# A tuned cross-attention and feed-forward kernel: the short chunk of the score maxima taken out of the score loop, with a new order in the opening

## The chip, the cores and the metric

The kernel runs on one core of one Trainium2 chip. The metric is the device time of one execution in microseconds (us), as the median of several runs; lower is better. A core has a matrix engine (TensorE, in profiles PE, with its weight loads as PEld), a vector engine (VectorE, DVE), an engine for activation functions (ScalarE, ACT), a general engine (GpSimd, POOL) and SyncE (SP), which issues transfers. Each works through its own list of instructions in order and waits on semaphores for the others.

## The reference

`x` has 2048 rows of 256, the context 1601 rows of 192 with a mask, and there are 16 heads of 64. A null key and a null value are put in front, so there are 1602 keys. All is float32.

```python
x = layer_norm(x, g_norm)                  # of a layer norm of the input
q = x @ Wq
k, v = jnp.split(context @ Wkv, 2, axis=-1)
...
k = jnp.concatenate([nk, k], axis=2)       # null key and value in front
v = jnp.concatenate([nv, v], axis=2)
sim = jnp.einsum('bhid,bhjd->bhij', q * sqrt_scale, k * sqrt_scale)
sim = jnp.where(full_mask[:, None, None, :], sim, max_neg)
attn = jax.nn.softmax(sim, axis=-1)
out = jnp.einsum('bhij,bhjd->bhid', attn, v)
...
return layer_norm(out @ Wout, g_out)
```

The result is added to `x`, and then a feed-forward part with three layers of signs (256 twice to 1024, 1024, 256; ReLU between) of a layer norm of the sum is added as well.

## The kernel before

Two heads form a pair, and 512 rows of `x` a block: 8 pairs times 4 blocks are 32 *units*, numbered u = 4p + b. Keys lie in 13 tiles of 128 (`KC`), the last of them with 66 rows. Every engine's list is written out by hand in program order (`manual_schedule`), so a line's place in the code is its place in the queue of its engine.

A unit has three stretches.

- **The score loop** (L709 to L722), k = 0 to 12. `exps` computes transposed scores of one key tile for both heads (`scores`, L442: two matmuls of a 64-row half of the array each, each in two fp32 passes) and ScalarE takes the exponential (L468). For k = 0 and 1 a matmul L466 puts in the shifts, later tiles build on the scores before them in the same PSUM buffer through stepped keys (`keys_stepped`). There are two score buffers (`spare`, the pool `ps_s`). In the same step one chunk of the row maxima of the *next* unit is computed: `max_chunk` multiplies 128 queries with 512 keys for both heads in fp32r (L400) and VectorE reduces (L403). Four query tiles times three chunks make 12 of these, and the thirteenth is the short chunk `REST`: the last 66 keys for all four query tiles, eight matmuls of 64 rows and 66 columns (L384) and one reduce (L387). `order` puts it into step 11. The maxima use the other PSUM pool with two buffers (`flex`, the pool `ps_f`), which also holds `den`, `mt`, the projections of queries, keys and values and, in the first units, the turned input. GpSimd sums the exponentials into `acc` (L720, L722, L728). A copy of one element of the last unit's `acc` on ScalarE (L711, `seen`) stands in step 2 or 8; ScalarE goes no further before that `acc` is complete.
- **The weighted sum** (L752, L475): 104 matmuls in four column groups. Ahead of it stand the denominators of the unit before, in the form of four quarters (`denominators`, L499, and `divided_quarters`), or within it in the whole form (`divided`, L524) in units 1, 30 and 31. GpSimd adds the remaining exponentials to `acc`.
- **The tail** (L782 to L800): the maxima are turned (`max_turned`, L413), the unit before is projected to the output (`project_out`, L488; VectorE adds it into `y_sb`, L491 and L493, which frees the buffer `po`), the queries of the unit after next are projected (`project_q`, L211, with ScalarE writing `qr` and `qT`, L212 and L213), and a quarter of the next pair's keys and values (`project_k`, L270 and L275; `project_v`, L305 and L320). `round_k` (L289) makes the fp32r copy `kr` of the keys for the maxima.

Each unit's maxima must be complete a unit ahead, since its shifts come from them.

Before the first unit, the *opening* (L566 to L678) loads everything, normalises blocks 0 and 1 of `x`, projects the first pair's keys, queries and values and computes the maxima of unit 0. Blocks 2 and 3 are normalised in units 0 and 1 (`input_normed` with `centred_beside`, ScalarE), for `input_turned` in the tail of the same unit. `masked_counted` (L425) computes `spent`, by which ScalarE scales the first exponentials' rows (L726). After the last unit the feed-forward part follows (L836, L867).

Of the kernel before, what the change touches and what calls it, by code (L numbers as in the profile page):

```python
# [38 lines left out]
def xattn_ffn(ctx, tc, x, ctxT, mask, g_norm, null_kv, wq, wkv, wout, g_out, k0, k1, k2, s0, s1, s2, out):  # L39
# [108 lines left out]
    with ExitStack() as att:  # L148
# [17 lines left out]
        mcol = ap.tile([128, 128], F32, name="mcol")  # L166
        pick = ap.tile([128, 4, 1], F32, name="pick")
# [66 lines left out]
        def first_keys(n, get, part=None):  # L234
# [3 lines left out]
            if part != 1:  # L238
                halves["k"] = get(f"psk_0_{n}")
# [6 lines left out]
            if part == 0:  # L246
                return
# [5 lines left out]
            for i, (start, w) in enumerate(chunks):  # L253
                for part in range(2 if n == 0 else 1):
                    keys = ds(256 * part, 256) if n == 0 else ds(start, w)
                    relative(kT, ps[:, i, ts(part, 256)] if n == 0 else ps[:, i, :w], keys)
                    if n == 0 and part == 0:
# [6 lines left out]
        def project_k(p, m):  # L264
# [3 lines left out]
            ps = flex(f"psk_{p}_{m}")  # L268
            for i in range(2):
                nc.tensor.matmul(  # L270
                    ps[:, i, :w], weights[p][1][:, 0, :], ctx_a[:, ds(start + i * w, w)], start=True, stop=False
                )
            for i in range(2):
# [10 lines left out]
        def round_k(p, m):  # L284

            kT, _, kr = pairs[p]
            start, w = HALF_KEYS[m]
            keys = ds(start, 2 * w)
            nc.scalar.copy(kr[:, keys], kT[:, keys])  # L289

# [8 lines left out]

        def values_begun(p, m, tiles, get=flex):  # L300
# [3 lines left out]
            for t in tiles:  # L304
                nc.tensor.matmul(  # L305
                    halves[p, m][:, t - 8 * m, :],
                    ctx_a[:, ts(t, 128)],
                    weights[p][1][:, 1, :],
                    start=t % 4 == 0,
# [4 lines left out]
        def values_ended(p, m):  # L314
# [3 lines left out]
            for t in sorted(tiles, key=lambda t: (t % 4, t)):  # L318
                rows = ts((t - 8 * m) // 4, 64)
                nc.tensor.matmul(  # L320
                    pv[:, t - 8 * m, :],
# [6 lines left out]
            w = len(tiles)  # L328
            nc.scalar.copy(v[:, ds(8 * m, w), :], pv[:, :w, :])
# [46 lines left out]
        def max_chunk(p, b, n, get=flex):  # L376
            ps = get(f"max_{p}_{b}_{n}")
            qr, kr = queries[p, b][1], pairs[p][2]
            if n == REST:
                start, w = CHUNKS[3]  # L380
                for t in range(4):
                    for j in range(2):
                        rows = ts(j, DH)
                        nc.tensor.matmul(  # L384
                            ps[:, j, ts(t, w)], qr[rows, ts(t, 128)], kr[rows, ds(start, w)], start=True, stop=True
                        )
                nc.vector.tensor_reduce(  # L387
                    maxima[p, b][:, :, :, 3].rearrange("p t j -> p j t"),
                    ps[:, :, : 4 * w].rearrange("p j (t k) -> p j t k", k=w),
# [5 lines left out]
            if n == 0:  # L395
                maxima[p, b] = wp.tile([128, 4, 2, 4], F32, tag="mx", name=f"mx_{p}_{b}")
# [167 lines left out]
        order = (*range(REST - 1), REST, REST - 1)  # L564
# [56 lines left out]
        nc.gpsimd.memset(mcol, 0.0)  # L621
        nc.gpsimd.memset(kept, 0.0)
# [331 lines left out]
```

## Time and profile before

| what | value |
|---|---|
| median of 3 runs | 1270.56 us (1269.84 to 1270.65) |
| time of the profiled execution | 1270.18 us |
| its span, first to last instruction | 1268.4 us |
| clock granted to TensorE | 1.0 |
| attention units, first score of unit 0 to the end of unit 31's weighted sum | 31.1 to 1079.0 us |
| four consecutive units (first score of unit 5 to that of unit 9) | 132.1 us |
| bytes moved by DMA | 13.46 MB |

How such lines are read: in a group of instructions or in a timeline, a line names the start, the length, the engine, the line of the kernel, the operation, output and inputs with their shapes and how many instructions were merged ("x4"). In square brackets stands how long the engine had been idle before, and what ended the wait. "64\*128" is the part of the array that a matmul uses, rows by columns. A merged line's length runs from its first start to its last end, so that the difference between starts says more of a rate than a length does. All times are in microseconds from the first instruction. DMA plays no part after the first 20 us.

```profile
PE   8999999999999999999999999999999999999998
POOL 5898999899889988998899988998898999701100
DMA  6000000000000000000000000000000010000000
```

These are rows of the page that cuts the span into 40 equal slices, with each digit the busy share in tenths: TensorE and GpSimd are busy throughout the attention units, DMA only at the start.

### The profile page before, as it was taken

How to read it: one execution, taken by the hardware profiler on the slowest of the kernel's cores; microseconds unless marked ns; L12 is line 12 of the kernel's file. 1: busy time of each engine (PE TensorE's matmuls, PEld its weight loads, DVE VectorE, ACT ScalarE, POOL GpSimd, SP SyncE). 2: the span in 40 equal slices, each digit the busy share in tenths (PEclk: the TensorE clock that was granted, in tenths of full speed). 3: DMA queues.
4: the chain of work that ended last, by engine and by line, in shares of the span. 5: the costliest groups of instructions: out<-in, count | busy, mean ns of one | idle time of the engine just before them, and what ended most of it. 6: DMA issues, size and time to landing. Idle time of an engine off the chain costs nothing.

```text
span 1268.4 us, 19642 instructions
## 1 busy us (share of the span) xinstructions
PE 1257.9 (99%) x8332; PEld 644.0 (51%) x8332; DVE 761.7 (60%) x812; ACT 717.9 (57%) x982; POOL 1008.5 (80%) x515
## 2 busy tenths in 40 slices
PE   8999999999999999999999999999999999999998
PEld 5344444444444444444444444444444443788887
DVE  6687766656665566556655666656666793635431
ACT  4776666666666656665666566666666676322120
POOL 5898999899889988998899988998898999701100
PEclk9999999999999999999999999999999999999999
DMA  6000000000000000000000000000000010000000
GB/s 171 1 1 5 1 1 13 5 1 1 13 5 1 1 14 5 1 1 13 5 1 2 13 5 1 1 1 6 1 17 1 1 42 1 1 17 1 17 17 17
DMA packets 16984, 13.46 MB, mean 11 GB/s; under 512 B 3152, under 2 KB 16336, under 8 KB 16896
## 3 DMA queue, kind: packets, MB, share of 16 engines
q1 hardware_dynamic: 15904, 11.21, 3.2%
q8 instruction: 65, 1.06, 0.4%
q10 hardware_dynamic: 656, 0.79, 0.2%
q0 software_dynamic: 336, 0.21, 0.1%
q14 instruction: 23, 0.19, 0.0%
HBM read 10.11 MB, written 2.10 MB: 10 GB/s over the span
## 4 chain that ended last, share of the span: by engine, by line
PE 95%; POOL 2%; ACT 1%; DMA 1%; issue 0%; DVE 0%; SPq 0%; DVEq 0%; POOLq 0%; ACTq 0%
PE sT L442 28%; PE av L475 27%; PE ps L836 12%; PE max L400 7%; PE psq L211 4%; PE po L488 4%; PE ps L867 2%; PE psv L305 2%; PE psk L270 1%; PE den L499 1%; PE sT L466 1%; PE psv L320 1%; POOL acc L728 1%; PE psk L275 1%; PE max L384 1%; PE mt L413 1%
## 5 line engine op out<-in xcount | busy, mean ns | idle before, releaser
L403 DVE TENSOR_REDUCE mx<-max 128x2 f32<-128x1024 f32 x384 | 444.4, 1218 | 86.0 <-PE max L400 82.3
L728 POOL TENSOR_TENSOR acc<-acc,e 128x1024 f32<-128x1024 f32 x192 | 473.1, 2464 | 15.1
L468 ACT ACTIVATE e<-sT 128x1024 f32<-128x1024 f32 x416 | 425.8, 1024 | 87.7 <-PE sT L466 44.3
L442 PE MATMUL sT<-qT,kT 64*128 64x512 f32 x1664 | 444.8, 608 | 1.6 <-ACT e L468 1.3
L722 POOL TENSOR_TENSOR acc<-acc,e 128x1024 f32<-128x1024 f32 x160 | 379.3, 2371 | 12.6
L475 PE MATMUL av<-e,v 128*32 128x512 f32 x3328 | 363.6, 592 | 0.1
L400 PE MATMUL max<-kr,qr 64*128 64x512 f32 x768 | 280.6, 718 | 1.2 <-ACT qr L227 1.0
L475 PEld LDWEIGHTS av<-e,v 128*32 128x32 f32 x3328 | 107.4, 110 | 237.9 <-issue 230.1
L442 PEld LDWEIGHTS sT<-qT,kT 64*128 64x128 f32 x1664 | 134.0, 185 | 132.6 <-ACT e L468 121.0
L720 POOL TENSOR_TENSOR acc<-e,e 128x1024 f32<-128x1024 f32 x32 | 75.6, 2363 | 59.6 <-ACT e L468 59.6
L400 PEld LDWEIGHTS max<-kr,qr 64*128 64x128 f32 x768 | 76.7, 187 | 88.6 <-DVE mx L403 65.2
L517 ACT COPY aoT<-r 32x256 f32<-32x256 f32 x224 | 90.2, 403 | 33.4 <-DVE r L511 31.1
L782 ACT COPY avs<-av 128x512 f32<-128x512 f32 x32 | 18.8, 587 | 145.8 <-PE av L475 145.8
L415 DVE TENSOR_TENSOR mT<-mt,pick 128x512 fp32r<-128x512 f32 x32 | 22.1, 690 | 113.4 <-PE mt L413 112.9
L518 DVE TENSOR_TENSOR aoT<-avs,aoT 128x512 f32<-128x512 f32 x28 | 33.3, 1189 | 94.4 <-ACT aoT L517 94.4
L836 PE MATMUL ps<-h0hi,w 128*128 128x512 f32 x256 | 79.6, 392 | 0.0
L836 PE MATMUL ps<-h0lo,w 128*128 128x512 f32 x256 | 78.9, 389 | 0.0
L124 POOL TENSOR_TENSOR y_sb<-y_sb,gout_sb 128x256 f32<-128x256 f32 x12 | 9.3, 777 | 85.6 <-DVE y_sb L91 85.6
L824 ACT ACTIVATE h1hi<-ps 128x1024 fp32r<-128x1024 f32 x16 | 16.4, 1027 | 99.2 <-PE ps L836 99.2
L212 ACT ACTIVATE qr<-psq 128x512 fp32r<-128x512 f32 x31 | 18.5, 598 | 93.5 <-PE psq L211 91.4
L488 PE MATMUL po<-wo,aoT 128*128 128x256 f32 x256 | 60.5, 379 | 0.0
L825 DVE SCALAR_TENSOR_TENSOR h1lo<-ps,h1hi 128x1024 fp32r<-128x1024 f32 x16 | 19.6, 1224 | 67.0 <-ACT h1hi L824 67.0
(171 smaller groups left out, 1207.8 us busy)
## 6 DMA issues: line engine op xcount, KB each, us to landing
out_x<-o SPq DMA_DIRECT2D x7, 256.0 KB, 2.1
x_sb<-in_x SPq DMA_DIRECT2D x3, 512.0 KB, 5.2
wa<-in_wkv SPq DMA_DIRECT2D x8, 128.0 KB, 2.9
wb<-in_wkv SPq DMA_DIRECT2D x16, 64.0 KB, 2.5
wq<-in_wq SPq DMA_DIRECT2D x8, 128.0 KB, 2.2
wo<-in_wout SPq DMA_DIRECT2D x8, 128.0 KB, 2.1
xnT<-in_k SPq DMA_DIRECT2D x1, 1024.0 KB, 5.7
ctx_a<-in_ctxT SPq DMA_DIRECT2D x2, 256.0 KB, 6.2
```

What stands on the lines that cost most here:

```text
L211: nc.tensor.matmul(ps[:, 0, :], weights[p][0][:, c, :], xnT[:, b, c, :], start=c == 0, stop=c == 1)
L400: nc.tensor.matmul(ps[:, j, :w], qr[rows, ts(t, 128)], kr[rows, ds(start, w)], start=True, stop=True)
L403: nc.vector.tensor_reduce(maxima[p, b][:, t, :, c], ps[:, :, :w], AX.X, ALU.max)
L442: nc.tensor.matmul(ps[:n, j, :], kT[rows, ds(128 * KEY_TILES[k], n)], qT[rows, :], start=k < 2, stop=k >= 2, skip_group_check=k >= 2,)
L468: nc.scalar.activation(e, ps, AF.Exp)
L475: nc.tensor.matmul(av[ts(i, 32), 0, :], v[:n, KEY_TILES[k], ts(i, 32)], e[:n, i // 2, :], start=k == 1, stop=k == 0, tile_position=(0, 32 ...
L488: nc.tensor.matmul(pv[:, t, :], aoT[:, ts(t, 128)], weights[p][3], start=True, stop=True)
L517: nc.scalar.copy(aoT[ds(64 * j + 32 * rows, 32), ts(h, 256)], r[ds(64 * j + 32 * h, 32), :])
L720: nc.gpsimd.tensor_tensor(acc, es[1], es[2], ALU.add)
L722: nc.gpsimd.tensor_tensor(acc, acc, es[k], ALU.add)
L728: nc.gpsimd.tensor_tensor(acc, acc, es[k], ALU.add)
L836: nc.tensor.matmul(ps[:, f, :], w(c)[:, ts(2 * g + f, 128)], parts[part][:, c, :], start=i == 0, stop=i == len(steps) - 1,)
```

## The change

- **The short chunk.** A tile `apart` per pair parity holds the last 66 keys of both heads in block-diagonal form: head 0 in rows 0 to 63 and columns 0 to 65, head 1 in rows 64 to 127 and columns 66 to 131, zeros elsewhere. The short chunk is then four matmuls of 128 rows and 132 columns. It leaves the score loop: it is computed one unit earlier, in the tail, straight after the projection of the queries that it needs (behind the output projection from unit 2 on, between the two halves of the key projection in units 0 and 1). In the loop step 0 has chunk 0, step 1 none, and step k from 2 on chunk k - 1. `round_k` leaves these 66 keys out of `kr` and `keys_apart` fills `apart`.
- **The tail's order.** From unit 2 on the queries are projected before the output.
- **Balanced last values.** The five last tiles of the values lie as three and two over the two halves of the PSUM tile (`places`), so that the second part of their projection takes three tiles in the upper and two in the lower row half, instead of four and one; the copy to `v` becomes two.
- **Blocks 2 and 3** of the input are centred on GpSimd within the sums of units 0 and 1, instead of on ScalarE.
- **The copy L711** stands in step 2 in all units from 1 to 28, instead of units 3 to 27; unit 1 takes the quartered denominators.
- **The opening.** One part of the key projection moves ahead of the second block's sums and the third maximum, six of eight value tiles are begun before the maxima of chunk 1, `reciprocal` and `second_normed` move behind three of these, the load of the Exp table moves behind the values, and `masked_counted` moves to the end of unit 0's loop.

```diff
+        apart = [ap.tile([128, 2, KEYS - CHUNKS[3][0]], F32R, name=f"apart_{i}") for i in range(2)]
...
-            keys = ds(start, 2 * w)
+            keys = slice(start, min(start + 2 * w, CHUNKS[3][0]))
             nc.scalar.copy(kr[:, keys], kT[:, keys])
+            if m == 1:
+                keys_apart(p, nc.scalar.copy)
+
+        def keys_apart(p, copy):
+
+            start, w = CHUNKS[3]
+            for j in range(2):
+                copy(apart[p % 2][ts(j, DH), j, :], pairs[p][0][ts(j, DH), ds(start, w)])
...
+        places = {t: t if t < 8 else t - 8 if t < 11 else t - 7 for t in range(KC)}
...
-            for t in sorted(tiles, key=lambda t: (t % 4, t)):
-                rows = ts((t - 8 * m) // 4, 64)
+            for t in sorted(tiles, key=lambda t: (places[t] % 4, t)):
+                rows = ts(places[t] // 4, 64)
...
-            w = len(tiles)
-            nc.scalar.copy(v[:, ds(8 * m, w), :], pv[:, :w, :])
+            for at, w in ((0, 8),) if m == 0 else ((8, 3), (11, 2)):
+                nc.scalar.copy(v[:, ds(at, w), :], pv[:, ds(places[at], w), :])
...
             if n == REST:
-                start, w = CHUNKS[3]
+                w = 2 * CHUNKS[3][1]
                 for t in range(4):
-                    for j in range(2):
-                        rows = ts(j, DH)
-                        nc.tensor.matmul(
-                            ps[:, j, ts(t, w)], qr[rows, ts(t, 128)], kr[rows, ds(start, w)], start=True, stop=True
-                        )
+                    nc.tensor.matmul(
+                        ps[:, t // 2, ts(t % 2, w)],
+                        qr[:, ts(t, 128)],
+                        apart[p % 2].rearrange("p j k -> p (j k)"),
+                        start=True,
+                        stop=True,
+                    )
...
-        order = (*range(REST - 1), REST, REST - 1)
...
+        for i in range(2):
+            nc.gpsimd.memset(apart[i].bitcast(F32), 0.0)
...
+        first_keys(1, spare, 0)
         mv, r = second_summed()
         max_chunk(0, 0, 6)
-        first_keys(1, spare, 0)
+        first_keys(1, spare, 1)
         max_chunk(0, 0, 9)
-        first_keys(1, spare, 1)
-        values_begun(0, 0, range(0, 8), spare)
+        first_keys(1, spare, 2)
+        values_begun(0, 0, range(0, 6), spare)
         max_chunk(0, 0, 1)
+        max_chunk(0, 0, 4)
+        values_begun(0, 0, range(6, 8), spare)
+        values_ended(0, 0)
+        max_chunk(0, 0, 7)
         nc.vector.reciprocal(r, r)
         second_normed(mv, r)
-        nc.scalar.activation(warm, eps_sb, AF.Exp)
-        max_chunk(0, 0, 4)
-        values_ended(0, 0)
-        max_chunk(0, 0, 7)
         first_keys(3, spare)
         max_chunk(0, 0, 10)
+        max_chunk(0, 0, 2)
         values_begun(0, 1, range(8, KC), spare)
-        max_chunk(0, 0, 2)
+        max_chunk(0, 0, 5)
         values_ended(0, 1)
-        max_chunk(0, 0, 5)
+        nc.scalar.activation(warm, eps_sb, AF.Exp)
...
-        project_q(0, 1, spare)
+        project_q(0, 1, spare, 0)
         max_chunk(0, 0, REST)
+        project_q(0, 1, spare, 1)
...
+        max_chunk(0, 1, REST)
         scores(0, 0, 0, sT[0])
-        masked_counted(flex)
...
-                    if k == (2 if 2 < u < len(units) - 4 else 8) and last is not None:
+                    if k == (2 if u < len(units) - 3 else 8) and last is not None:
...
-                    if nxt is not None:
-                        max_chunk(*nxt, order[k])
+                    if nxt is not None and k != 1:
+                        max_chunk(*nxt, max(k - 1, 0))
...
+                if u == 0:
+                    masked_counted(flex)
...
+                if u < 2:
+                    mv, r = input_root(u + 2)
+                    nc.vector.reciprocal(r, r)
+                    nc.scalar.activation(warm, eps_sb, AF.Exp)
                 for k in (0, *range(8, KC)):
                     nc.gpsimd.tensor_tensor(acc, acc, es[k], ALU.add)
+                    if k == 0 and u < 2:
+                        for j in range(4):
+                            t = 4 * (u + 2) + j
+                            nc.gpsimd.tensor_scalar(
+                                y_sb[:, t, :], x_sb[:, t, :], mv[:, j, 0:1], r[:, j : j + 1], ALU.subtract, ALU.mult
+                            )
...
-                if u < 2:
-                    input_normed(u + 2, *input_root(u + 2), beside=True)
-                    nc.scalar.activation(warm, eps_sb, AF.Exp)
...
-                quarters = last is not None and u not in (1, len(units) - 2, len(units) - 1)
+                quarters = last is not None and u not in (len(units) - 2, len(units) - 1)
...
+                if u >= 2 and u + 2 < len(units):
+                    project_q(*units[u + 2])
                 if last is not None:
                     project_out(*last[:2], aoT)
-                if u + 2 < len(units):
+                if u < 2:
                     project_q(*units[u + 2])
+                if u + 2 < len(units) and u >= 2:
+                    max_chunk(*units[u + 2], REST)
                 if p + 1 < NP:
 
-                    (project_k if b < 2 else project_v)(p + 1, b % 2)
+                    if u < 2:
+                        project_k(p + 1, b, 0)
+                        max_chunk(*units[u + 2], REST)
+                        project_k(p + 1, b, 1)
+                    else:
+                        (project_k if b < 2 else project_v)(p + 1, b % 2)
```

More of the change, by code (lines that the diff above doesn't have):

```diff
@@ L237, in first_keys @@
             chunks = (CHUNKS[1], CHUNKS[2]) if n == 1 else (CHUNKS[n],)
-            if part != 1:
+            if not part:
                 halves["k"] = get(f"psk_0_{n}")
@@ L245, in first_keys @@
                     )
-            if part == 0:
+            if part in (0, 1):
                 return
@@ L256, in first_keys @@
                     relative(kT, ps[:, i, ts(part, 256)] if n == 0 else ps[:, i, :w], keys)
-                    if n == 0 and part == 0:
+                    if n == 3:
+                        keys_apart(0, nc.gpsimd.tensor_copy)
+                    elif n == 0 and part == 0:
                         nc.scalar.copy(kr[:, keys], kT[:, keys])
@@ L262, in first_keys, with project_k @@
                 nc.vector.memset(kT[:, KEYS:], 0.0)
-        def project_k(p, m):
+        def project_k(p, m, part=None):
             kT = pairs[p][0]
             start, w = HALF_KEYS[m]
-            ps = flex(f"psk_{p}_{m}")
-            for i in range(2):
+            if part != 1:
+                halves["k"] = flex(f"psk_{p}_{m}")
+            ps = halves["k"]
+            for i in range(2) if part != 1 else ():
                 nc.tensor.matmul(
@@ L272, in project_k @@
                 )
+            if part == 0:
+                return
             for i in range(2):
@@ L305, in values_begun @@
                 nc.tensor.matmul(
-                    halves[p, m][:, t - 8 * m, :],
+                    halves[p, m][:, places[t], :],
                     ctx_a[:, ts(t, 128)],
                     weights[p][1][:, 1, :],
-                    start=t % 4 == 0,
+                    start=places[t] % 4 == 0,
                     stop=False,
@@ L317, in values_ended @@
             tiles = range(8 * m, min(8 * m + 8, KC))
-            for t in sorted(tiles, key=lambda t: (t % 4, t)):
-                rows = ts((t - 8 * m) // 4, 64)
+            for t in sorted(tiles, key=lambda t: (places[t] % 4, t)):
+                rows = ts(places[t] // 4, 64)
                 nc.tensor.matmul(
-                    pv[:, t - 8 * m, :],
+                    pv[:, places[t], :],
                     ctx_b[rows, ts(t, 128)],
@@ L378, in max_chunk @@
             qr, kr = queries[p, b][1], pairs[p][2]
+            if (p, b) not in maxima:
+                maxima[p, b] = wp.tile([128, 4, 2, 4], F32, tag="mx", name=f"mx_{p}_{b}")
             if n == REST:
-                start, w = CHUNKS[3]
+                w = 2 * CHUNKS[3][1]
                 for t in range(4):
-                    for j in range(2):
-                        rows = ts(j, DH)
-                        nc.tensor.matmul(
-                            ps[:, j, ts(t, w)], qr[rows, ts(t, 128)], kr[rows, ds(start, w)], start=True, stop=True
-                        )
+                    nc.tensor.matmul(
[5 more added lines that the diff above has]
+                    )
                 nc.vector.tensor_reduce(
-                    maxima[p, b][:, :, :, 3].rearrange("p t j -> p j t"),
-                    ps[:, :, : 4 * w].rearrange("p j (t k) -> p j t k", k=w),
+                    maxima[p, b].rearrange("p (i t) j c -> p i (t j) c", i=2)[:, :, :, 3],
+                    ps[:, :, : 2 * w].rearrange("p i (t k) -> p i t k", k=w // 2),
                     AX.X,
@@ L394, in max_chunk @@
             t, c = divmod(n, 3)
-            if n == 0:
-                maxima[p, b] = wp.tile([128, 4, 2, 4], F32, tag="mx", name=f"mx_{p}_{b}")
             start, w = CHUNKS[c]
```

## The prediction

> **What bounds the kernel now.** I read the page first: busy shares and the chain that ended last.
>
> ```profile
> PE 1257.9 (99%) x8332; PEld 644.0 (51%) x8332; DVE 761.7 (60%) x812; ACT 717.9 (57%) x982; POOL 1008.5 (80%) x515
> PE 95%; POOL 2%; ACT 1%; DMA 1%; issue 0%; DVE 0%; SPq 0%; DVEq 0%; POOLq 0%; ACTq 0%
> ```
>
> TensorE carries the chain, but its ends are modelled, so 99% does not say it runs at full rate. Start times do. Every unit has three stretches: the score loop (13 steps), the weighted sum (104 matmuls, 0.109 us apart, 11.3 us), and a tail of projections. Next I read the timeline of unit 5 (pair 1, block 1), first the middle of its loop.
>
> ```profile
> 205.59 4.44 ACT L468 ACTIVATE e<-sT 128x1024 f32<-128x1024 f32 x4
> 205.88 4.61 DVE L403 TENSOR_REDUCE mx<-max 128x2 f32<-128x1024 f32 x4
> 206.66 0.30 PEld L442 LDWEIGHTS sT<-qT,kT 64*128 64x128 f32 x4 [0.36 <-ACT e L468]
> 207.20 0.19 PEld L400 LDWEIGHTS max<-kr,qr 64*128 64x128 f32 x2 [0.23 <-DVE mx L403]
> 207.82 0.30 PEld L442 LDWEIGHTS sT<-qT,kT 64*128 64x128 f32 x4 [0.43 <-ACT e L468]
> 208.91 0.30 PEld L442 LDWEIGHTS sT<-qT,kT 64*128 64x128 f32 x4 [0.36 <-ACT e L468]
> ```
>
> Every score load L442 waits for an exponential, two steps back, because there are two score buffers. Load starts alternate 1.16 and 1.09 apart, 2.25 for two steps. That is the sum of one closed chain: exponential 1.02, 0.05 to the load, load 0.11, two passes of 0.43, then 0.21 until the next exponential in that buffer: 2.25. The maxima of a step (one pass, 0.21) run while TensorE would wait, and are not in the chain. VectorE is as full by coincidence: its reduces start 1.13 apart without a gap. Which of the two sets the pace is told by unit 31, which computes no maxima at all; its exponentials:
>
> ```profile
> 1054.14 2.01 ACT L468 ACTIVATE e<-sT 128x1024 f32<-128x1024 f32 x2 [0.30 <-PE sT L466]
> 1056.46 2.01 ACT L468 ACTIVATE e<-sT 128x1024 f32<-128x1024 f32 x2 [0.30 <-POOL acc L728]
> 1058.77 2.01 ACT L468 ACTIVATE e<-sT 128x1024 f32<-128x1024 f32 x2 [0.30 <-POOL y_sb L699]
> 1061.08 1.02 ACT L468 ACTIVATE e<-sT 128x1024 f32<-128x1024 f32 x1 [0.30 <-PE sT L442]
> ```
>
> Two steps still take 2.31. So the loop is bound by the chain of exponential and scores, not by maxima on TensorE or VectorE. Third, the place where the short chunk stands now (step 11):
>
> ```profile
> 212.33 0.30 PEld L442 LDWEIGHTS sT<-qT,kT 64*128 64x128 f32 x4 [0.43 <-ACT e L468]
> 212.89 0.94 PE L384 MATMUL max<-kr,qr 64*128 64x66 f32 x8
> 213.29 0.42 PEld L384 LDWEIGHTS max<-kr,qr 64*128 64x128 f32 x6 [0.24 <-issue]
> 213.62 0.31 PEld L442 LDWEIGHTS sT<-qT,kT 64*128 64x128 f32 x4
> 213.86 0.71 DVE L387 TENSOR_REDUCE mx<-max 128x8 f32<-128x528 f32 x1
> ```
>
> The load of step 12 comes 1.29 after that of step 11 and shows no wait: here alone the maxima hold TensorE. The loads go two by two, about 0.11 a pair, 0.44 in all: the halves already run side by side. The reduce starts 0.31 after the last matmul starts, which leaves room for the load and a stream of some 0.03 (66 columns at the one-pass rate 0.213/512), not for 0.11. Last, the tail:
>
> ```profile
> 226.82 1.89 PE L488 MATMUL po<-wo,aoT 128*128 128x256 f32 x8
> 228.55 1.88 PE L211 MATMUL psq<-xnT,wq 128*128 128x512 f32 x4
> 230.26 1.51 PE L270 MATMUL psk<-ctx_a,wa 128*128 128x400 f32 x4
> 231.70 0.94 PE L275 MATMUL psk<-ctx_b,wb 64*128 64x400 f32 x4
> 232.48 1.02 PE L442 MATMUL sT<-qT,kT 64*128 64x512 f32 x4
> ```
>
> The starts are 1.73, 1.71, 1.44, 0.78 apart, against 1.71, 1.71, 1.34, 0.67 of pure streaming: no hole. What is put here is paid in full.
>
> **The change, part by part** (against the profiled execution: span 1268.4, time 1270.18, which stands 0.4 below the median 1270.56).
>
> *Short chunk out of 31 loops.* Step 12's load then waits for exponential 10 only (212.34 + 1.02 + 0.05 = 213.41 instead of 213.62): 0.20 each, -6.2. Nothing more comes from step 1 having no chunk: exponential 2 cannot start before exponential 1 and the copy L711 (0.92 + 0.17 = 1.09 behind it, which is today's spacing), and exponential 3 follows 1 by the chain. Bounds: 0, and 1.1 if the loop (first score matmul to `den`, 199.63 to 214.93) fell from 15.3 to TensorE's own sum (13 x 0.854 + 14 x 0.213 = 14.1) and some 0.1 of load; I take 0.20, by unit 31.
>
> *Short chunk in 30 tails.* Four full-height loads at the 0.11 of a load pair = 0.446, streams (132 columns, 0.055) hidden under them; the new order (queries, output, short chunk) hides the wait for `qr`, ready 0.8 after the queries, under the 1.73 of the output projection. Its reduce (0.6) lies in VectorE's idle tail. Units 0 to 27: 28 x 0.446 = +12.5. Bounds of one: 0.22 (streams alone), 0.88 (two fp32 passes of 0.11, four times). Units 28 and 29 have no key or value projection behind it. Today the queries' 1.71 covers the add of `po` into `y_sb` (L493, 0.2 to start, 1.22 long), which frees the buffer of the next scores; moved in front, they cover nothing, and the scores start 1.47 after `po` instead of 0.10 after the queries: +1.37 each, +2.7.
>
> The Trainium skill (TensorE: Matmul & The Clock Gate, Part 3, The mechanism) says that a weight load overlaps running matmuls only in a different row group. By this the full-height form would lose what the halves have, 0.107 + 0.055 a matmul, 0.65 a chunk, and the time would be 5.7 higher. The rows speak against the rule: L488's full-height matmuls start 0.216 apart, with streams of 0.213, so their loads are hidden.
>
> *Last values balanced.* The upper row half takes three tiles instead of four: 2 passes x 0.11 = 0.22 saved in seven tails: -1.5. The copy split in two stays under the 0.8 that the first scores and shifts need.
>
> *Opening.* The key projection of chunk 1 fills TensorE's wait for `qr` (idle 0.47 before 14.16), the first maximum of chunk 1 moves from 20.18 to about 19.4 (behind the POOL cast, itself behind `sums` at 18.45), and VectorE runs its reduces unbroken from there. The Exp table load (1.28 + 0.20) moves to just ahead of the `xnT` scalings, which then start near 28.15 instead of 28.02 and hold the queries. `second_normed` moves three reduces back, and with it GpSimd's key steps, to about 30.7; the third scores, the first to need them, come near 35. With the extra short chunk (0.44) and without the count (0.32) the first shifts come at 33.65 instead of 34.11: -0.45. The count returns at the end of loop 0, +0.33. Net -0.1; bounds -1.5 and +1.
>
> *At nothing:* two clearings of `apart` (0.25 each by L621) before GpSimd's first cast, which has 3 us idle ahead of it; the two small copies into `apart` (about 0.25 each, by L260) once a pair on ScalarE, in the 4.4 us it idles before the copy of `av` (L782), and twice on GpSimd in the opening. Without that cover: 0.5 each time, 4 in all.
>
> *Units 0 to 2.* GpSimd gains four scalings (2.17 by L356) between sums; ScalarE loses eight operations of 0.5 that lay beside the weighted sum (0). What they cost is lateness of `acc`:
>
> ```profile
> 40.53 12.17 POOL L722 TENSOR_TENSOR acc<-acc,e 128x1024 f32<-128x1024 f32 x5
> 52.77 16.18 POOL L728 TENSOR_TENSOR acc<-acc,e 128x1024 f32<-128x1024 f32 x6
> ```
>
> From exponential 2 of unit 0 (36.99 today): six sums end at +15.7, the count's three small ones +0.95, ScalarE's scaling of `e` 1.15 (it now waits for `spent` behind the sums), one sum 2.4, scalings 2.2, five sums 12.2: `acc` ends at +34.7 to +35.2. The copy L711 of unit 1, moved from step 8 to step 2, would come at +33.15 (today's 31.24 + 0.92, less 0.20, plus 0.33, short chunk 0.39, and 0.47 below). Behind it on ScalarE stand all exponentials, and so the chain: +1.8 (bounds 0.5 and 2.8). In units 0 and 1 the keys' PSUM buffer is the one that the next loop's first maxima take, which wait for the second `kT` write (1.18 long, 0.22 behind the projection): 0.47, twice, +0.9. Unit 1's quartered denominators: first score to the weighted sum's end 27.12 as in unit 2 instead of 27.83, -0.7. The early copy in units 2 and 28 gives the spacing of the other units (first score to first weighted matmul 15.94 against 15.76, and 16.36 against 15.97): -0.6.
>
> Sum: -6.2 + 12.5 + 2.7 - 1.5 - 0.1 + 1.8 + 0.9 - 0.7 - 0.6 = **+8.8**, so 1270.2 + 8.8 = **1279.0**.
>
> **Rivals.** *The loop speeds up (faster).* If VectorE's unbroken 1.13 is what paces the loop, then twelve reduces (13.6) no longer do, and it falls toward 14.2, 1.1 below today's, instead of 0.20: 31 x 0.9 = 28 off, 1251; half of that, 1265. It is faster from 0.37 more per loop on. For it: the gapless reduces. Against: unit 31, and the wait on the exponential at each score load. *The short chunk costs more in the tail*: at 0.65 to 0.88 each, 28 x 0.2 to 0.43 more, 1285 to 1291. Against: the 0.31 at the reduce. *Most of it is hidden*: 0.22 each (-6.3), and no stall in unit 1: 1271, no change. For it: the streams take only 0.055; against: the loads' pitch. *GpSimd is late in every unit*: today its sum ends 0.8 us ahead of the copy L711 in the first unit of a pair, 1.8 in the others. If that were lost by 1 us seven times, 1286. Against: the interval in which it stands changes by -0.20 + 0.45 - 0.22, nothing, and no work is added after unit 1.
>
> **How the numbers follow.** Differences under 0.2% (2.5 us) can't be told from none. Forecast (slower, 1274 to 1284) 0.66; dearer short chunk or a late GpSimd 0.12; hidden 0.09; faster loop 0.13. So slower 0.78, same 0.09, faster 0.13. The range 1272 to 1287 holds the forecast with the opening's and the stall's bounds, and the lower part of the dear case.
>
> **What would show it.** Right: exponentials 2 to 10 keep 2.25 per two steps; step 12 starts 0.2 earlier; four L402 matmuls 0.11 apart in the tail; unit 1's exponential 2 stands behind the copy of `acc` for one to three us; units 29 and 30 open with a wait for `y_sb`; ordinary units last 0.2 to 0.3 longer, those after block 3 the same. Wrong: steps at 1.07 to 1.10 each, or L402 matmuls 0.16 or more apart.

## The result, and the profile after

The changed kernel takes **1293.6 us** (median of 5 runs, 1293.5 to 1295.5), the kernel before 1270.6 us (1269.8 to 1272.5) beside it: ratio **1.0182**, 95% interval 1.0168 to 1.0196. It is slower, as forecast, but by 23 us and not by 8.8, and so outside the range of 1272 to 1287. The profiled executions differ by as much: span 1292.4 after, 1268.4 before, +24.0.

The busy shares and the chain of the changed kernel, which answer to the first two lines shown of before:

```profile
PE 1267.1 (98%) x8208; PEld 661.8 (51%) x8208; DVE 752.2 (58%) x810; ACT 714.0 (55%) x996; POOL 1017.6 (79%) x526
PE 69%; DVE 23%; POOL 5%; ACT 1%; issue 1%; DVEq 0%; POOLq 0%; ACTq 0%
```

The busy shares say nothing: TensorE has 98% instead of 99%. The chain does. VectorE, which had 0% of it, now has 23%. The list of TensorE's waits in the changed kernel (engine, waiting tile and line, releaser; total us, times, longest) names the place:

```profile
PE den L519 <- DVE mx L423: 10.1, 29, 0.4
PE sT L462 <- ACT e L488: 3.0, 7, 1.0
PE xT L576 <- POOL y_sb L762: 2.1, 3, 0.8
```

The denominators `den` wait for the maxima `mx` in 29 units, 0.35 us each on average. In the kernel before this wait is absent. Here is the end of unit 5's loop before, in the timeline (start, duration, engine, line, operation, tiles; in brackets the idle time before it and what ended it):

```profile
210.40 3.47 DVE L403 TENSOR_REDUCE mx<-max 128x2 f32<-128x1024 f32 x3
215.03 1.23 DVE L403 TENSOR_REDUCE mx<-max 128x2 f32<-128x1024 f32 x1 [0.46 <-PE max L400]
...
213.65 1.11 PE L442 MATMUL sT<-qT,kT 64*128 64x512 f32 x4
214.19 0.80 PE L400 MATMUL max<-kr,qr 64*128 64x512 f32 x2
214.93 0.64 PE L499 MATMUL den<-acc,ones 128*32 128x256 f32 x8
```

and the same place after:

```profile
218.87 6.87 DVE L423 TENSOR_REDUCE mx<-max 128x2 f32<-128x1024 f32 x6
...
223.14 1.02 PE L462 MATMUL sT<-qT,kT 64*128 64x512 f32 x4
223.60 0.80 PE L420 MATMUL max<-kr,qr 64*128 64x512 f32 x2
224.75 0.64 PE L519 MATMUL den<-acc,ones 128*32 128x256 f32 x8 [0.36 <-DVE mx L423]
225.18 2.35 PE L495 MATMUL av<-e,v 128*32 128x512 f32 x20
```

There are two PSUM buffers named `f`, and maxima and `den` take them in turn (L49), so `den` takes the one of the chunk at step 11. Before, that was the short chunk, reduced in 0.71; VectorE was idle for 0.46 after it, and `den` followed the maxima of step 12 by 0.74. After, it is chunk 10: it is the last but one of six reduces without a pause (1.22 each, 1.13 from start to start), ends at 224.61, and `den` follows the maxima of step 12 by 1.15. From the first scores to `den` unit 5 takes 15.52 (209.23 to 224.75) where it took 15.30 (199.63 to 214.93). Step 12 does start earlier in the unit, 13.91 after the first scores (209.23 to 223.14) against 14.02, but the loop as a whole is 0.22 longer where it should have been 0.20 shorter: 0.42 lost in each unit.

The starts of the first scores (timelines) split the 24.0 by stretch:

| stretch | before | after | difference | predicted |
|---|---|---|---|---|
| start to exponential 2 of unit 0 | 36.99 | 37.94 | +0.95 | -0.45 |
| to the first scores of unit 3 | 96.94 | 104.47 | +7.53 | +2.87 |
| units 3 to 27 | 825.05 | 840.16 | +15.11 | +4.65 |
| unit 28 to the end of the span | 309.42 | 309.86 | +0.44 | +1.7 |

(The last column regroups the prediction's terms: 0.246 for each unit's chunk, moved from the loop to the tail, -0.22 for each tail with balanced values, -0.2 and -0.4 for the early copies in units 2 and 28.)

The tail itself is as forecast. Unit 5's end, after:

```profile
236.65 1.88 PE L213 MATMUL psq<-xnT,wq 128*128 128x512 f32 x4
238.37 1.89 PE L508 MATMUL po<-wo,aoT 128*128 128x256 f32 x8
239.90 0.75 PE L402 MATMUL max<-apart,qr 128*128 128x132 f32 x4
240.49 1.56 PE L276 MATMUL psk<-ctx_a,wa 128*128 128x400 f32 x4
241.98 0.94 PE L283 MATMUL psk<-ctx_b,wb 64*128 64x400 f32 x4
```

From the end of the weighted sum's row (236.55, before 226.72) to the next first scores it lasts 6.21 against 5.76, +0.45, for a forecast of 0.446, and there is no wait in it.

Units 0 to 2 lose by GpSimd. Its timeline around the end of unit 0, with ScalarE's copy in unit 1 that waits for it:

```profile
55.85 2.37 POOL L758 TENSOR_TENSOR acc<-acc,e 128x1024 f32<-128x1024 f32 x1 [1.25 <-ACT e L752]
58.21 6.43 POOL L762 TENSOR_SCALAR y_sb<-x_sb,mv_x,rstd_x 128x256 f32<-128x256 f32 x4
64.62 12.08 POOL L758 TENSOR_TENSOR acc<-acc,e 128x1024 f32<-128x1024 f32 x5
...
76.74 0.19 ACT L735 COPY seen<-acc 1x1 f32<-1x1 f32 x1 [1.24 <-POOL acc L758]
76.83 1.91 ACT L488 ACTIVATE e<-sT 128x1024 f32<-128x1024 f32 x2
```

The four scalings take 6.43, not the 2.2 forecast. The operations on this tile (minimum, median, maximum of one, in ns) show that the row the forecast used, L356 of before (L374 here), is not their price:

```profile
L762 POOL TENSOR_SCALAR y_sb<-x_sb,mv_x,rstd_x x8: 1209/1222/2827, 58.2 to 98.6; 128x256 f32<-128x256 f32 x8
L374 POOL TENSOR_SCALAR y_sb<-x_sb,sums,rstd_x x4: 554/556/558, 24.4 to 26.0; 128x256 f32<-128x256 f32 x4
```

Same size, same engine, but L374 adds and multiplies, and L762 subtracts and multiplies.

Something else slows the tail of unit 0. After three waits of TensorE for these scalings (0.61 to 0.77) the clock granted to TensorE is 0.5 from 65.47 to 68.89, and the query projection takes 3.34 from its first start to that of the key projection (65.80 to 69.14), where it took 1.82 in the kernel before (61.57 to 63.39):

```profile
65.80 3.50 PE L213 MATMUL psq<-xnT,wq 128*128 128x512 f32 x4 [0.56 <-ACT xnT L577]
69.14 1.51 PE L276 MATMUL psk<-ctx_a,wa 128*128 128x401 f32 x4
```

In the kernel before the granted clock is 1.0 from 4.5 to 1267.4.

### The profile page after: what moved, and what is told of

Read it like the earlier page. It is cut to its first block, busy times and chain, and to the rows that moved or that the text cites. A ratio compares the mean times of both kernels' runs of the same rounds, so it can differ in the third digit from the quotient of the medians.

```text
span 1292.4 us, 19425 instructions
## 1 busy us (share of the span) xinstructions
PE 1267.1 (98%) x8208; PEld 661.8 (51%) x8208; DVE 752.2 (58%) x810; ACT 714.0 (55%) x996; POOL 1017.6 (79%) x526
## 4 chain that ended last, share of the span: by engine, by line
PE 69%; DVE 23%; POOL 5%; ACT 1%; issue 1%; DVEq 0%; POOLq 0%; ACTq 0%
PE av L495 26%; DVE mx L423 22%; PE ps L878 11%; PE sT L462 10%; PE po L508 4%; PE psq L213 4%; PE ps L909 2%; POOL acc L758 2%; PE max L420 2%; PE psv L323 2%; POOL acc L746 2%; PE den L519 1%; PE psk L276 1%; PE sT L486 1%; PE psv L338 1%
## 5 line engine op out<-in xcount | busy, mean ns | idle before, releaser
L420 PE MATMUL max<-kr,qr 64*128 64x512 f32 x768 | 291.4, 751 | 2.0 <-POOL kr L264 1.0
L495 PEld LDWEIGHTS av<-e,v 128*32 128x32 f32 x3328 | 128.2, 110 | 216.2 <-issue 210.5
L537 ACT COPY aoT<-r 32x256 f32<-32x256 f32 x232 | 93.4, 403 | 36.0 <-DVE r L531 33.6
L538 DVE TENSOR_TENSOR aoT<-avs,aoT 128x512 f32<-128x512 f32 x29 | 30.4, 1049 | 97.7 <-ACT aoT L537 97.7
L513 DVE TENSOR_TENSOR y_sb<-po,y_sb 128x1024 f32<-128x1024 f32 x28 | 34.3, 1224 | 68.4 <-PE po L508 68.4
L508 PE MATMUL po<-wo,aoT 128*128 128x256 f32 x256 | 60.5, 379 | 0.0
```

The costliest lines, as they stand in the source:

```text
L420: nc.tensor.matmul(ps[:, j, :w], qr[rows, ts(t, 128)], kr[rows, ds(start, w)], start=True, stop=True)
L495: nc.tensor.matmul(av[ts(i, 32), 0, :], v[:n, KEY_TILES[k], ts(i, 32)], e[:n, i // 2, :], start=k == 1, stop=k == 0, tile_position=(0, 32 ...
L508: nc.tensor.matmul(pv[:, t, :], aoT[:, ts(t, 128)], weights[p][3], start=True, stop=True)
L537: nc.scalar.copy(aoT[ds(64 * j + 32 * rows, 32), ts(h, 256)], r[ds(64 * j + 32 * h, 32), :])
```

## The experiments

The theory after this reading: three separate losses, each at a place where a wait was not priced. (1) `den` waits for the reduce of the chunk at step 11; (2) GpSimd's dearer centring, and the copy moved ahead of it, hold units 0 to 2; (3) in the opening the exponential's table load holds the transposed input.

**e1: no chunk at step 11 instead of step 1.** One line of the changed kernel, so that `den` takes the buffer of chunk 10 two steps after it was filled:

```
-if nxt is not None and k != 1:   max_chunk(*nxt, max(k - 1, 0))
+if nxt is not None and k != 11:  max_chunk(*nxt, min(k, 11))
```

> The changed kernel, but the step without a chunk of maxima is step 11 instead of step 1 (steps 0 to 10 have chunks 0 to 10, step 12 has chunk 11). Theory (the denominators' matmuls stand behind the reduce of chunk 10, whose PSUM buffer they take): the wait of L519 on the reduces, 10.1 us in the changed kernel, falls to under 1, and the time falls by about 10, to 1283 to 1285. Rival (VectorE's reduces pace the whole loop, and the wait only shows it): the time stays within 2 us of 1293.6.

Measured 1282.4 us (1282.0 to 1282.7), ratio to before 1.0092 (1.0077 to 1.0107): 11.2 less than the changed kernel. The end of unit 5's loop:

```profile
222.01 0.80 PE L420 MATMUL max<-kr,qr 64*128 64x512 f32 x2
222.74 0.64 PE L519 MATMUL den<-acc,ones 128*32 128x256 f32 x8
...
216.16 5.74 DVE L423 TENSOR_REDUCE mx<-max 128x2 f32<-128x1024 f32 x5
222.85 1.23 DVE L423 TENSOR_REDUCE mx<-max 128x2 f32<-128x1024 f32 x1 [0.95 <-PE max L420]
```

VectorE has a pause again, `den` comes 0.73 after the maxima, and the wait is not in the list of waits any more. First scores to `den` is 15.09, which is 0.21 under before: the prediction's 0.20. Units 3 to 27 take 829.66, 4.61 more than before, where the prediction's terms give 4.65.

**e9: the kernel before, with the short chunk one step earlier.** The same claim from the other side, with none of the change's other parts:

```
-order = (*range(REST - 1), REST, REST - 1)
+order = (*range(REST - 2), REST, REST - 2, REST - 1)
```

> The kernel before with nothing changed but the place of the short chunk in a unit's loop: at step 10 instead of step 11, so that chunk 10 comes at step 11 and chunk 11 stays at step 12. Theory: the denominators at the end of the loop take the PSUM buffer of the chunk at step 11, whatever it is; in the kernel before that is the short chunk, whose reduction is short. With chunk 10 there TensorE waits 0.35 us for VectorE at the denominators of some 29 units, as in the changed kernel: 1279.5 to 1281.5 us, with the wait 'den' for 'mx' in the profile at about 10 us. Rival: the wait belongs to the changed kernel's other moves (the chunks one step later, the queries ahead of the output's projection): within 0.7 us of 1270.5.

Measured 1279.3 us (1279.1 to 1281.2), ratio 1.0068 (1.0052 to 1.0084). The wait appears in the old kernel:

```profile
PE den L499 <- DVE mx L403: 9.0, 28, 0.3
```

0.32 each instead of the 0.35 expected, and 8.6 us for a mere exchange of two steps. That settles (1): what counts is which chunk stands at step 11.

**e2: GpSimd's centring as an addition.** VectorE negates the four means once (a new small tile `nm`), and GpSimd adds:

```
-... x_sb[:, t, :], mv[:, j, 0:1], r[:, j : j + 1], ALU.subtract, ALU.mult
+... x_sb[:, t, :], nm[:, j : j + 1], r[:, j : j + 1], ALU.add, ALU.mult
```

> The changed kernel, but GpSimd centres blocks 2 and 3 by adding a negated mean (one more small VectorE instruction) instead of subtracting the mean; shapes, operands and place stay. Theory (the subtracting form itself takes 1.21 us on GpSimd where the adding one takes 0.56): eight instructions at about 0.56, the waits of the transposes L576 on GpSimd (2.1) gone, the sums of unit 0 complete 3 to 4 us earlier, the time 4 to 6 lower, 1287.5 to 1289.5. Rival (they are slow because of what runs beside them): they stay at 1.2 and the time at 1293.6 within 1.

Measured 1291.6 us (1290.0 to 1291.8), ratio 1.0161 (1.0144 to 1.0178): 2 less, between the two expectations. The price of one did fall, as the tile's operations show:

```profile
L764 POOL TENSOR_SCALAR y_sb<-x_sb,nmx,rstd_x x8: 552/558/2047, 57.4 to 93.1; 128x256 f32<-128x256 f32 x8
```

TensorE's waits for the centred rows at the transposes went with it, and unit 0 (first scores to first scores) takes 35.20 instead of 39.36. But unit 1 now starts early enough to run into the copy, on ScalarE:

```profile
69.35 1.02 ACT L488 ACTIVATE e<-sT 128x1024 f32<-128x1024 f32 x1 [0.30 <-PE sT L486]
73.13 0.19 ACT L735 COPY seen<-acc 1x1 f32<-1x1 f32 x1 [2.76 <-POOL acc L760]
```

Its loop (first scores to the weighted sum) takes 20.27 instead of 17.16. The clock shows it too: it stays 1.0 in the tail of unit 0, but is 0.5 from 75.75 to 79.16, behind TensorE's wait of 2.50 that this stall causes. Most of what the tail gave, unit 1 took back.

**e3: the centring back on ScalarE**, where the kernel before has it, as eight operations beside the weighted sum; the four scalings on GpSimd and the early root are left out:

```
-    if u < 2:  mv, r = input_root(u + 2) ... gpsimd.tensor_scalar(...)
+    if u < 2:  input_normed(u + 2, *input_root(u + 2), beside=True); warm
```

> The changed kernel, but blocks 2 and 3 are centred on ScalarE again, as in the kernel before. Theory (GpSimd's scalings make its sums late): the sums of units 0 and 1 end 4 to 6 us earlier and the copy of acc in units 1 and 2 waits under 0.5 us; but ScalarE starts its eight operations only behind spent, some 4 us later than in the kernel before, so that the transposes of units 0 and 1 wait for it 1 to 3 us: 1287 to 1291. Rival (GpSimd is late for the other work that it got): the time stays within 1 us of 1293.6.

Measured 1292.6 us (1291.0 to 1292.9), ratio 1.0170 (1.0154 to 1.0185): 1 less, near the rival. GpSimd's sum of unit 0 ends at 71.51 instead of 76.70 and the copy's stall is gone (unit 1's loop 15.95), but its list of waits has others that the changed kernel's has not, or not so long (2.0 us of `psq` L213 for ScalarE's `xnT` L577, 1.3 of `po` L508 for `aoT` L538). Behind the wait of 2.0 the granted clock is 0.5 again, from 64.97 to 68.38. Moving the centring to another engine moves the wait; what holds these two was not tried.

**e5: e2, and the early copy only from unit 3 on.**

```
-if k == (2 if u < len(units) - 3 else 8) and last is not None:
+if k == (2 if 2 < u < len(units) - 3 else 8) and last is not None:
```

> The changed kernel with GpSimd's centring as an addition of the negated mean (as in the run with that alone, 1291.6 us), and with the early copy of the end of the running sum (step 2 of a unit) used only from unit 3 on; units 1 and 2 copy at step 8, as before. Theory: with the cheaper centring what is left of units 0 to 2 is one stall: the copy in unit 1 waits for GpSimd until 73.13 us and holds exponential 2 behind it, so that unit 1's loop takes 20.27 us where 15.95 is usual. The copy at step 8 takes that away: 4.3 us less, 1286.5 to 1288.5 us. Rival: GpSimd's lateness is what counts and only shows at the copy; the running sum of unit 1 is then late for unit 2's denominators instead, and the time stays within 1.5 us of 1291.6.

Measured 1288.1 us (1287.9 to 1289.5), ratio 1.0141 (1.0126 to 1.0157): 3.5 less than e2, 5.5 less than the changed kernel. ScalarE in unit 1 no longer stops for the copy, which comes at 77.32, when the sum has long been complete:

```profile
69.58 1.95 ACT L488 ACTIVATE e<-sT 128x1024 f32<-128x1024 f32 x2 [0.30 <-PE sT L486]
...
77.32 0.17 ACT L735 COPY seen<-acc 1x1 f32<-1x1 f32 x1
```

The rival, that GpSimd's lateness only moves on, falls by its own number: the sum of unit 0 ends at 73.36, no earlier than in e2 (73.10), and unit 2's loop takes 16.10, near the 15.95 of e2. The clock stays 1.0 throughout, so the 5.5 us hold the price of the slow clock as well.

**e6: the table load back behind the centring of block 1.**

```
         second_normed(mv, r)
+        nc.scalar.activation(warm, eps_sb, AF.Exp)
...
         values_ended(0, 1)
-        nc.scalar.activation(warm, eps_sb, AF.Exp)
```

> The changed kernel with the load of the table for the exponential back in its old place in the opening, right after the centring of block 1 and ahead of the last keys (the change had put it behind the values). Theory: ScalarE is idle there for 3.6 us, so the load is free, and the transposed input no longer waits for it: TensorE's idle 1.25 us at the second half of the queries goes, and the whole takes 1.0 to 1.3 us less than the changed kernel, 1292.3 to 1292.6 us. Rival: the copies of the values, or what follows them, hold TensorE at the same point anyway: within 0.4 us of 1293.6.

Measured 1292.9 us (1292.6 to 1294.0), ratio 1.0178 (1.0164 to 1.0192): 0.7 less, short of the 1.0 to 1.3 expected. The ranges of the two kernels' runs overlap, so the total alone would not show it. ScalarE and TensorE in the opening of the changed kernel:

```profile
27.24 0.75 ACT L347 COPY v<-psv 128x384 f32<-128x384 f32 x2 [3.59 <-PE psv L338]
28.01 1.28 ACT L685 ACT_TABLE_LOAD   x1
...
29.41 0.67 ACT L577 ACTIVATE xnT<-xT,gn_sb 128x512 f32<-128x512 f32 x1
...
30.13 1.12 PE L203 MATMUL psq<-xnT,wq 128*128 128x512 f32 x2 [1.25 <-ACT xnT L577]
```

and of e6:

```profile
23.50 1.28 ACT L679 ACT_TABLE_LOAD   x1
...
27.09 0.75 ACT L347 COPY v<-psv 128x384 f32<-128x384 f32 x2 [2.10 <-PE psv L338]
```

The load fits into an idle stretch. One has to know how late the input was to compare openings: ScalarE's first work on block 1 of `x`, which waits for its transfer, starts between 15.9 and 17.0 in these profiles, whatever the kernel. Exponential 2 of unit 0 follows that moment by 20.77 before (36.99 after 16.22), by 20.90 in the changed kernel (37.94 after 17.04), by 19.99 in e6 (36.86 after 16.87). The distance belongs to the opening and not to the run: it is 20.72 to 20.78 in the four profiles with the old opening, 20.90 to 20.94 in the five with the changed one, and 20.00 in e11, which has that of e6. So of the changed opening's +0.95, 0.82 is a late transfer in that one profile, and its own share is +0.13; with the load mended it gains 0.8.

**e4: the short chunk in its old form**, eight matmuls of 64 rows instead of four of 128, in the tails and in the opening:

```
-for t in range(4):  matmul(..., qr[:, ts(t, 128)], apart[p % 2] (2 x 66 columns))
+for t in range(4):  for j in range(2):
+    matmul(..., qr[ts(j, DH), ts(t, 128)], apart[p % 2][ts(j, DH), j, :])
```

> The changed kernel, but the short chunk is computed in its new place in the old form: eight matmuls of 64 rows and 66 columns instead of four of 128 rows and 132. Theory (a pair of half-height matmuls costs what one of full height does, 0.11): the short chunk takes 0.44 to 0.55 in the tail and the time stays within 2 us of 1293.6 (a switch of the array's form in each tail may add 0.1, some 3 in all). Rival (the full-height form is the dear part): 1288 or lower.

Measured 1302.1 us (1301.9 to 1304.0), ratio 1.0250 (1.0235 to 1.0266): 8.5 more, where the theory expected at most 3 and the rival a gain. The tail of unit 5:

```profile
238.93 1.89 PE L509 MATMUL po<-wo,aoT 128*128 128x256 f32 x8
240.75 0.63 PE L403 MATMUL max<-apart,qr 64*128 64x66 f32 x8
241.31 1.61 PE L276 MATMUL psk<-ctx_a,wa 128*128 128x400 f32 x4
```

The chunk starts 1.82 after the output projection; in the changed kernel it is 1.53 (238.37 to 239.90). The tail lasts 6.52 instead of 6.21, and the opening is 0.5 longer (exponential 2 comes 21.43 after the input).

**e10: the same form, but from unit 2 on behind the projection of keys or values**, next to the scores, which are matmuls of 64 rows too:

```
-if u + 2 < len(units) and u >= 2:  max_chunk(*units[u + 2], REST)
 if p + 1 < NP:  ... project_k or project_v ...
+if u + 2 < len(units) and u >= 2:  max_chunk(*units[u + 2], REST)
```

> The changed kernel with the short chunk in the old half-height form (as in the run at 1302.1 us), but in the tails of units 2 to 29 behind the projection of keys or values, right ahead of the next unit's first scores, instead of ahead of it. Theory: the half-height form streams half as many columns (0.2 us against 0.4 us a chunk); what made it dear is the change between matmuls of 128 rows and of 64 rows on both its sides. Behind the projection, whose last matmuls have 64 rows as the scores have, there is no change more than without it: a tail costs 0.2 to 0.25 us less than in the changed kernel, 28 tails 5.6 to 7 us, 1286.5 to 1288.0 us. Rival: eight matmuls with eight weight loads are dear as such: within 2 us of 1302.1.

Measured 1294.4 us (1294.2 to 1294.7), ratio 1.0184 (1.0169 to 1.0199): 7.7 less than e4, but 0.8 more than the changed kernel instead of 5.6 to 7 less. Half of the theory holds. The place takes away the 0.29 of e4, which was no wait for another engine (tail of unit 5: 6.12 instead of 6.52), so the change between 128 and 64 rows is the likely cause. The other half falls: the narrow form is hardly cheaper for streaming half as much.

```profile
240.87 0.94 PE L283 MATMUL psk<-ctx_b,wb 64*128 64x400 f32 x4
241.34 0.84 PE L403 MATMUL max<-apart,qr 64*128 64x66 f32 x8
242.01 1.11 PE L463 MATMUL sT<-qT,kT 64*128 64x512 f32 x4
```

The starts of the matmuls after the first are 0.11 apart, pair by pair, with 66 columns, and in the changed kernel also 0.11 apart, one by one, with 132. So the columns do not set the pace; the weight loads, which start 0.11 apart as well, may.

The tails of units 3 to 27 are 2.1 shorter in all than in the changed kernel (6.12 for 6.21 in unit 5), but the loops behind them are 2.6 longer. Part of that is the effect of (1) again: with the short chunk last, the first maxima of the loop take the PSUM buffer of the projection, and behind a key projection their weight load waits for `kT` (0.37 in unit 6, starting 1.08 after the first scores instead of 0.86). The opening, where the narrow chunk still stands, adds 0.4 (21.35 after the input). So the form in its new place had a small gain, and other places took it.

**e11 and e12: all mended places together** (e1, e5 and e6), with the short chunk as the change has it, and with the form and place of e10.

> The changed kernel with the four mended places together and the short chunk as the change has it: no chunk at step 11 instead of step 1 (-11.2 us by itself), GpSimd's centring as an addition of the negated mean and the copy at step 8 in units 1 and 2 (-5.5 together), the exponential's table at its old place (-0.7). Theory: they are separate losses and add up, 1293.6 - 17.4 = 1276.2, 1275 to 1277.5 us; what is left over the kernel before is the short chunk's 0.25 us in a tail (0.45 less the loop's 0.20) in 28 units, 7 us, less the balanced values. Rival: the losses overlap, so that one mended place uncovers the next: 1279 or more.

> The same four mended places, and the short chunk in its half-height form behind the projection in the tails. Theory: 6.2 us less again, 1270 us (1269 to 1271.5): moving the chunk out of the loop is then neither gain nor loss, since it streams for 0.2 us in either place, and the balanced values (-1.5) pay for what the opening and units 0 to 2 still lose. Rival: within 1.5 us of the run with the full-height form.

Measured 1276.0 us (1275.7 to 1276.6), ratio 1.0041 (1.0027 to 1.0055), and 1276.6 us (1276.4 to 1277.5), ratio 1.0045 (1.0030 to 1.0060). The losses add up, 17.6 for 17.4 expected; e12's theory (1270) falls with that of e10. The granted clock stays 1.0 in both.

**e7 and e8: the kernel before with parts of the change.** e7 has only the balanced places of the last five values (the dictionary `places` and the copy in two parts); e8 has these and the early copy also in units 2 and 28:

```
-(2 if 2 < u < len(units) - 4 else 8)
+(2 if 1 < u < len(units) - 3 else 8)
```

> The kernel before with one part of the change alone: the last five values of each pair placed three and two to a PSUM bank instead of four and one, copied by two copies instead of one. The prediction's step gives -1.5 us in all (1269.0 us); the rival, that ScalarE's second copy gives it back or that the matmuls are covered, gives 1270.5 +- 0.4.

> The kernel before with the two parts of the change that the prediction priced as gains and that need nothing else: the balanced places of the last values, and the early copy of the end of the running sum also in units 2 and 28 (not in unit 1, where GpSimd is late). Prediction's steps: -1.5 for the places and -0.6 for the copies, 1268.4 us, better than both kernels by more than a measurement's uncertainty only if both hold. Rival: unit 2 waits for the running sum at step 2 as unit 1 does, and loses 0.5 to 1 us there: 1269.0 to 1270.0.

Measured 1269.1 us (11 runs; ratio 0.9988, 0.9980 to 0.9997) and 1268.7 us (11 runs; ratio 0.9987, 0.9978 to 0.9996), beside 1270.5 (21 runs). Both are a little faster than the kernel before, e8 by 0.13%: the intervals leave out 1, but only just, and the totals do not tell e7 from e8. In the trace of e7 each unit of block 3 is 0.22 shorter from first scores to first scores (32.41 against 32.63), and units 3 to 30 take 1.65 less; in e8 unit 2's loop falls from 15.94 to 15.75, and unit 28's from 16.36 to 15.96 (16.14 already in e7, for no known reason). e8 has the lowest time of all versions run.

## Why the prediction was right in direction and wrong in size

- **"Short chunk out of 31 loops ... 0.20 each": right, and undone.** The step that failed stands in the same paragraph: *"Nothing more comes from step 1 having no chunk."* It asked what later exponentials could gain and not which buffer each later instruction takes. With no chunk at step 1 all chunks stand one step later, chunk 10 comes where the short chunk was, and `den` inherits its reduce. The prediction's fences even held both facts: the 0.71 reduce of the short chunk, and VectorE's reduces 1.13 apart without a gap. It read the gapless row as *"full by coincidence"*, since only a wait at the scores was sought; the wait came at the next taker of the buffer. The gain itself is there: with the buffer put right the way to `den` is 0.21 shorter (e1). Price of the wait: 11.2 us (e1), confirmed on the old kernel by e9.
- **"Short chunk in 30 tails ... 0.446": right.** 0.45 measured. For the full-height form the prediction's rows held against the rule that it quoted: four loads 0.11 apart, not 0.65 a chunk.
- **Units 28 and 29, "+1.37 each": wrong, too dear.** Their tails grew by 0.39 each (3.64 to 4.03). The first scores of unit 29 start at 1014.14 while VectorE still reads `po` (until 1015.08), so they do not take its buffer. 1.9 us less than forecast.
- **Units 0 to 2: the late copy right, sizes wrong, and a wait and the clock left out.** *"ends at +34.7 to +35.2"* after exponential 2 was 38.8 (76.70 - 37.94), for *"scalings 2.2"* were 6.43. The copy did hold ScalarE, for 1.24. The transposes' wait for these scalings was not in the sum at all, nor the half clock behind it. e5 prices all of these together at 5.5 us; the prediction had 1.8 for the copy. Two smaller terms did not come either. *"0.47, twice, +0.9"*: in units 1 and 2 the weight load of the first maxima starts 0.86 after the first scores, as before, so there was no such wait. *"Unit 1's quartered denominators ... -0.7"*: in e11 unit 1 takes 26.94 to the end of its weighted sum instead of 27.99, but its tail 8.16 instead of 6.63, and the short chunk explains only some 0.45 of that.
- **The opening, "-0.45" to the first exponentials: close only by a cancellation.** Measured from the input's arrival it was +0.13. The gains were larger than forecast (0.8 in e6), but the table load, said to start the scalings *"near 28.15"*, put them at 29.41; that cost 0.7 (total of e6) to 0.9 (20.90 against 19.99).
- **Balanced values, "-1.5", and the early copies, "-0.6": right.** -1.4 and another -0.5 in e7 and e8 (the second within the noise of the totals; the two loops in the trace are 0.19 and 0.40 shorter than before).

Put together: the three losses measured in e1, e5 and e6, 17.4, taken from 1293.6 leave 1276. The prediction, without its 1.8 for a copy that e11 does not have and without the 1.9 too much for units 28 and 29, would be 1275.3. The direction was no luck, since e11 is still 5.4 us slower than before. That the total comes so close is luck in part: by the stretches of the table above e11 differs from before by -0.77, +1.86, +4.59 and -0.19, where the prediction without these two terms has -0.45, +1.07, +4.65 and -0.2: the loops and tails agree, the opening and units 0 to 2 miss in opposite directions. Of the rivals none was the one that came: a late VectorE at `den` was not among them.

Left open: whether the subtraction or the way its scalar is read makes GpSimd's price (e2 changed both), and the rest of what units 0 to 2 lose in e11. That unit 0 of e6 takes 40.63, longer than the 39.36 of the changed kernel, has its answer in the clock: it is 0.5 for 6.83 us there (63.54 to 70.36) instead of 3.41. Unit 1 gives it back: in e6 GpSimd's sum ends at 75.62, just before the copy is due, while in the changed kernel the copy waits for it until 76.70.

## What to carry to other kernels

When a step leaves a ring of buffers, everything behind it moves by one, and the next taker of a buffer inherits another predecessor: write down the order of takers before and after, and for each the release time of what it inherits, above all for the first taker behind the loop. An engine whose work runs without a gap beside the critical one deserves a second look: here it did not set the pace of the steps, but the first instruction that came to depend on one of its late pieces waited 0.35 us in each of 29 units. Take the price of an operation from a row with the same arithmetic and operands, and when an early copy or table load is moved, look first for what stands behind it on its engine. And look at the granted clock behind every new wait of TensorE: the wait's own length may not be its whole price.

## What the runs showed of the hardware that was not expected

- The granted TensorE clock was 0.5 for 3.41 us, in e6 and e10 for 6.83, shortly after waits of TensorE: three of 0.6 to 0.8 (the changed kernel, e1, e4, e6, e10) or one of 2.0 and 2.5 (e3, e2). In the seven profiles without such waits in units 0 to 2 it was 1.0 in all but the first and last few microseconds. Of e2's four runs the one with a mean clock of 1.0 took 1290.0, the others (0.998 and 0.999) 1291.6 to 1291.8. That the waits bring the clock down is inferred; no run tests it by itself.
- GpSimd's scaling of 128x256 f32 by two scalars of a partition took 1.22 us as subtract and multiply (the mean read in place from a tile of pairs) and 0.558 as add and multiply (from a tile of its own).
- The first of the four scalings in unit 0 took 2.83 (58.21 to 61.04) and in e2 2.05. In both VectorE was multiplying `ctx_a` by `keep`, two inputs in SBUF, until 59.91 (2.38 from 57.53) and 59.00: the remaining 1.13 and 0.43 are near the ordinary price. A plain sum on GpSimd did the same beside the same instruction: 4.00 in the kernel before (52.77 to 56.77, VectorE until 54.53) and 3.90 in e3 (57.90 to 61.80, VectorE until 59.58), where 2.36 is usual. The Trainium skill (SBUF — State Buffer, Who interferes with whom) says that a VectorE instruction with two inputs in SBUF contends with a GpSimd one that reads SBUF, and that the shared ports are an exclusive lock. These four rows agree.
- A group of matmuls of 64 rows between matmuls of 128 rows, in the middle of a tail, cost 0.31 us more than one of 128 rows (e4 against the changed kernel), nearly all of it ahead of the first narrow one; beside narrow neighbours the tail was 0.40 shorter (e10).
- Short matmuls that each need new weights start 0.11 apart, with 66 columns in a pair of half-height ones or 132 in a full one; halving the columns did not shorten the distance.
